# An encoder-decoder layer on one core: where the sum of the last half-size product of a slot stands among its matmuls

## The chip, the cores and the metric

The kernel runs on one core of one Trainium2 chip, as one launch in float32. The metric is device time in microseconds (us). A time is the median of several executions; a profile is one further execution, taken by the hardware profiler. Engines are named as the profile names them: PE is TensorE's matmul, PEld its weight load, DVE is VectorE, ACT is ScalarE, POOL is GpSimd, SP issues the DMAs. Each engine works through its own queue in program order and waits for others by semaphores.

## What is computed

One encoder layer over a short context and one decoder layer over a long sequence:

```python
B, T, S, D, H, DFF = 2, 2048, 77, 512, 16, 2048
def _mha(xq, xkv, w_in, b_in, w_out, b_out, bias):
    q, k, v = (heads(z) for z in (xq @ wq.T + bq, xkv @ wk.T + bk, xkv @ wv.T + bv))
    attn = softmax(q @ k.T / sqrt(hd) + bias)
    return merge(attn @ v) @ w_out.T + b_out
...
memory = encoder_layer(ctx_1024)
yn = _ln(y, dec_n1_s, dec_n1_b)
y = y + _mha(yn, yn, dec_sa_in_w, dec_sa_in_b, dec_sa_out_w, dec_sa_out_b, sb)
y = y + _mha(_ln(y, dec_n2_s, dec_n2_b), memory, dec_ca_in_w, ..., cb)
h = _ln(y, dec_n3_s, dec_n3_b)
y = y + (relu(h @ dec_ff1_w.T + dec_ff1_b) @ dec_ff2_w.T + dec_ff2_b)
```

The part that matters here is the causal self-attention of the decoder (sb is a relative bias plus the causal mask): its projections to q, k, v and its output projection are each a 512 x 512 weight applied to 512 tokens at a time.

## The kernel before

The sequence of each batch is cut into four blocks of 512 tokens, so there are eight blocks (b, m). The self-attention runs as a stream of units (b, m, g, t): a block, a group g of four heads and a tile t of 128 query tokens, 16 units a block and 128 in all. For each unit the scores (line 375) are made in pieces of up to 512 keys, DVE moves them out of PSUM while it takes their maxima (lines 384 and 391), ACT takes the exponentials (line 406), PE turns them (line 427), DVE and ACT copy the turned pieces out (lines 432 and 434), and PE multiplies them by the values (line 456).

All other work of that stage hangs on the units' slots, written out by hand: `jobs` (projections, run in the middle of a slot), `light` (before the jobs) and `late` (behind them). The function `slot(n)` issues them; `last[0]` is true while the last job of a slot is issued. The order in which instructions are issued is the order of each engine's queue; waits between engines are put in by the language that the kernel is written in, from what each instruction reads and writes. A job's weights are loaded to one of three buffers `wqk` a few jobs ahead, in the order of the jobs (`load_next`).

PSUM has eight banks of 512 columns, one tile `psum`. `bank()` hands them out in a ring, less one or so that is kept for the product with the values.

For a block with m > 0 the projections of q, k and v use seven products of half size in place of eight (a scheme of Strassen and Winograd's kind): the 512 x 512 problem is cut in four quarters; sums of weight quarters (S1 to S4) lie in DRAM, sums of token quarters (T1 to T4) are made by POOL. `PARTS` names what each product multiplies. Products are added up one on another in the quarters of the result:

| product | what its sum does |
| --- | --- |
| 1 | starts 11 (by ACT for k, v and output; by DVE with a bias for q) |
| 6 | 12 = 11 + product |
| 7 | 22 = 12 + product (with a step of the bias for q and k) |
| 4 | 21 = 22 + product |
| 2 | added to 11 |
| 5 | added to 12 and to 22 |
| 3 | added to 12 |

- `part_job(kind, b, m, i)` makes one product of k, v or the output ("o"). Its result is one PSUM bank in two halves of 256 columns: four matmuls on line 1134, two for each half (each shows as two records in the profile). Then come the sums, behind all four: lines 1141 and 1145 for product 1, and line 1150 where the job is the last of its slot (half by half, 256 columns each); lines 1155, 1159, 1161 and 1164 else (in one, 512 columns wide, but product 7 of k in two).
- `pair_job(b, m, h, parts)` makes two products of q, or product 3 alone, for the half h of its columns. The two products share a bank, 256 columns each: two matmuls for each on line 1049, and behind all of them the sums (lines 1055 to 1065).

The projections of the output for seven of the eight blocks are part jobs of kind "o" in four slots: products 1 and 6; 7 and 4; 2 and 5; 3. The other slots are in a table, where a and b are the halves of q ("a25" is the pair of products 2 and 5 of half a) and the number is the slot relative to the block's first:

```python
-5: "a16 a74", -4: "k1 k6", -3: "k7 k4", -2: "k2 a25", -1: "k5 k3 a3", 0: "v1 v6", 1: "v7 v4 v2",
2: "v5 v3", 3: "b16", 4: "b74 b25", 5: "b3",
```

For m = 1 the first four rows are three: "k1 a16 k6", "a74 k7", "k4 k2 a25".

Of the kernel before, what the change touches and what calls it, by code (L numbers as in the profile page):

```python
# [54 lines left out]
def tile_encoder_decoder(ctx: ExitStack, tc: tile.TileContext, ins, out):  # L55
# [22 lines left out]
    def vec(name, i):  # L78
        c = _COL[name] + i
        return vecs[:, c : c + 1]  # L80
# [78 lines left out]
    with (  # L159
# [872 lines left out]
        def pair_job(b, m, h, parts):  # L1032

            def load():
                w = sb.tile([P, NC, P], F32, name="wqk", tag="wqk", bufs=3)
                for j, i in enumerate(parts):
                    src = saq_d[Q_OPS.index(PARTS[i][0])][:, ts(h, TOK)]
                    nc.sync.dma_start(w[:, 2 * j : 2 * j + 2, :], src.rearrange("p (k o) -> p k o", k=2))
                return w

            def run(w):
                if parts[0] == 1:
                    for g in (2 * h, 2 * h + 1):
                        qTs[b, m, g] = sb.tile([P, MB], F32, name="q", tag="q", bufs=3)
                mm = bank()
                for j, i in enumerate(parts):
                    n = of_nT(b, m, PARTS[i][1])
                    for c in range(2):
                        nc.tensor.matmul(mm[:, ts(j, TOK)], w[:, 2 * j + c, :], n[:, c, :], start=c == 0, stop=c == 1)  # L1049
                d = {  # L1050
                    f"{r + 1}{c + 1}": qTs[b, m, 2 * h + r][:, ts(c, TOK)] for r in range(2) for c in range(2)
                }
                got = [mm[:, ts(j, TOK)] for j in range(len(parts))]
                if parts == (1, 6):
                    ve.tensor_scalar(d["11"], got[0], qbias[:, 2 * h : 2 * h + 1], None, ALU.add)
                    ve.tensor_tensor(d["12"], got[1], d["11"], ALU.add)
                elif parts == (7, 4):
                    ve.scalar_tensor_tensor(d["22"], got[0], qstep[:, h : h + 1], d["12"], ALU.add, ALU.add)
                    ve.tensor_tensor(d["21"], got[1], d["22"], ALU.add)
                elif parts == (2, 5):  # L1060
                    for to, j in (("11", 0), ("12", 1), ("22", 1)):
                        ve.tensor_tensor(d[to], got[j], d[to], ALU.add)
                else:
                    assert parts == (3,)
                    ve.tensor_tensor(d["12"], got[0], d["12"], ALU.add)

            return load, run, True
        n_tiles, last = {}, [False]
        PARTS = {
            1: ("11", "11"), 2: ("12", "21"), 3: ("S4", "22"), 4: ("22", "T4"),  # L1070
            5: ("S1", "T1"), 6: ("S2", "T2"), 7: ("S3", "T3"),
        }
        ADDS = {2: ("11",), 3: ("12",), 5: ("22", "12")}

        def of_nT(b, m, name):
            if name[0] == "T":
                return n_tiles[b, m][int(name[1]) - 1].rearrange("p (c o) -> p c o", c=2)
            r, c = int(name[0]) - 1, int(name[1]) - 1
            return nTs[b, m][:, 2 * r : 2 * r + 2, ts(c, TOK)]
# [28 lines left out]
        def part_job(kind, b, m, i):  # L1108
            name, by = PARTS[i]

            def load():
                w = sb.tile([P, NC, P], F32, name="wqk", tag="wqk", bufs=3).rearrange("p c o -> p (c o)")
                w = w.rearrange("p (c o) -> p c o", c=2)
                if name[0] == "S":
                    src = sa_d[kind][int(name[1]) - 1].rearrange("p (c o) -> p c o", c=2)
                else:
                    src = quarter(sa_name[kind], int(name[1]) - 1, int(name[0]) - 1, sa_from[kind])
                nc.sync.dma_start(w, src)
                return w

            def place(to):
                r, c = int(to[0]) - 1, int(to[1]) - 1
                if kind == "k":
                    return kT[:, 2 * r : 2 * r + 2, m * MB + c * TOK : m * MB + (c + 1) * TOK]
                if kind == "o":
                    return wbt[:, 2 * c : 2 * c + 2, ts(r, TOK)]
                return vv[:, m * TB + 2 * c : m * TB + 2 * c + 2, ts(r, TOK)]

            def run(w):
                n, mm = of_o(b, m, by) if kind == "o" else of_nT(b, m, by), bank()  # L1130
                left, right = (w, n) if kind == "k" else (n, w)
                for f in range(2):
                    for c in range(2):
                        nc.tensor.matmul(  # L1134
                            mm[:, ts(f, TOK)], left[:, c, ts(f, P)], right[:, c, :], start=c == 0, stop=c == 1,
                        )
                got = mm.rearrange("p (f n) -> p f n", f=2)
                d = {to: place(to) for to in ("11", "12", "21", "22")}
                if i == 1 and kind == "k":
                    for f in range(2):  # L1140
                        nc.scalar.activation(
                            d["11"][:, f, :], got[:, f, :], AF.Identity, bias=vec("dec_sa_in_b", NC + f)
                        )
                elif i == 1:
                    nc.scalar.copy(d["11"], got)
                elif last[0] and not (i == 7 and kind == "k"):
                    for f in range(2):
                        for to in {6: ("12",), 7: ("22",), 4: ("21",)}.get(i) or ADDS[i]:
                            onto = {6: "11", 7: "12", 4: "22"}.get(i, to)
                            ve.tensor_tensor(d[to][:, f, :], got[:, f, :], d[onto][:, f, :], ALU.add)  # L1150
                elif i == 6:
                    ve.tensor_tensor(d["12"], got, d["11"], ALU.add)
                elif i == 7 and kind == "k":
                    for f in range(2):
                        ve.scalar_tensor_tensor(
                            d["22"][:, f, :], got[:, f, :], kstep[:, f : f + 1], d["12"][:, f, :], ALU.add, ALU.add
                        )
                elif i == 7:
                    ve.tensor_tensor(d["22"], got, d["12"], ALU.add)
                elif i == 4:  # L1160
                    ve.tensor_tensor(d["21"], got, d["22"], ALU.add)
                else:
                    for to in ADDS[i]:
                        ve.tensor_tensor(d[to], got, d[to], ALU.add)

            return load, run, True

# [19 lines left out]
        for x, (b, m) in enumerate(blocks):  # L1187
# [3 lines left out]
            if first:  # L1191
                jobs[max(u - 5, -1)].append(q_job(b, m, 0))
                jobs[max(u - 4, -1)].append(k_job(b, m, 0))
                for t, at in enumerate((u + 1, u + 2, u + 3, u + 4) if x else (-1, 1, 3, 4)):
                    jobs[at].append(v_job(b, m, t))
                jobs[u - 1 if x else 0].append(q_job(b, m, 1))
                jobs[u if x else 2].append(k_job(b, m, 1))
                for g, at, then in ((2, 3, 4), (3, 5, 6)) if x else ((2, 6, 7), (3, 8, 9)):
                    jobs[u + at].append(q_job(b, m, g))
                    jobs[u + then].append(k_job(b, m, g))  # L1200
            else:
                todo = {
                    -5: "a16 a74", -4: "k1 k6", -3: "k7 k4", -2: "k2 a25", -1: "k5 k3 a3", 0: "v1 v6", 1: "v7 v4 v2",
                    2: "v5 v3", 3: "b16", 4: "b74 b25", 5: "b3",
                } if x % NMB > 1 else {
                    -4: "k1 a16 k6", -3: "a74 k7", -2: "k4 k2 a25", -1: "k5 k3 a3", 0: "v1 v6", 1: "v7 v4 v2",
                    2: "v5 v3", 3: "b16", 4: "b74 b25", 5: "b3",
                }
                for at, names in todo.items():
                    for name in names.split():  # L1210
                        h, parts = "ab".find(name[0]), tuple(int(i) for i in name[1:])
                        jobs[u + at].append(
                            pair_job(b, m, h, parts) if h >= 0 else part_job(name[0], b, m, parts[0])
                        )
            if x == 0:
                jobs[NU + 5].append(fold_job())
            for t in range(TB):
                end = x == len(blocks) - 1
                out_at = u + NU + (2 if end else 7 if m == NMB - 1 else 6) + t
                if not end:  # L1220
                    if t:
                        continue
                    for k, part in ((0, 1), (0, 6), (1, 7), (1, 4), (2, 2), (2, 5), (3, 3)):
                        jobs[out_at + k].append(part_job("o", b, m, part))
                    late[out_at - 2].append(lambda b=b, m=m: out_sums(b, m))
                    late[out_at].append(lambda b=b, m=m: sum_n("T4", lambda n: of_o(b, m, n)))
# [767 lines left out]
```

## Time and profile before

| | us |
| --- | --- |
| median of 3 runs (2726.21 to 2733.03) | 2726.84 |
| the profiled execution | 2728.59 |
| its span | 2726.8 |

The span runs from the first to the last instruction of the program; the rest of the execution lies around it. The granted clock of PE over the profiled execution was 0.997. In the profile's rows "x8" is a count of instructions, the first number a start and the second a duration in timelines, and what stands in brackets is how long the engine was idle before and who released it. In lists by line, three numbers are the shortest, the median and the longest duration in ns. In lists of waits, the numbers are microseconds in total and how often. A duration that PE shows for a matmul reaches to its modelled end; matmuls overlap, so that the distance of their starts is what each costs.

The stages of the kernel as the trace has them: preparation to about 113 us, the self-attention with the encoder and the first block's cross-attention among it to about 1590 us, then the rest of the cross-attention and the feed-forward to the end.

### The profile page before, as it was taken

What the parts mean: (1) busy time and instruction counts of PE and PEld (TensorE: products, weight loads), DVE (VectorE), ACT (ScalarE), POOL (GpSimd) and SP (SyncE); (2) the same over time, 40 slices, a digit from 0 to 9 for tenths busy, and PEclk for the clock granted to TensorE, in tenths of its full rate; (3) what the DMA queues carried; (4) which work ended last, traced back from release to release, by engine and by line L of the source; (5) the groups of instructions that cost most, each with busy time, mean ns of one, the idle gap of its engine ahead of it and who ended that gap; (6) DMA issues with size and microseconds to landing.
All of it is one profiled execution on the core that took longest, in us unless ns stands there. A gap on an engine that the chain in (4) does not pass through costs nothing.

```text
span 2726.8 us, 68267 instructions
## 1 busy us (share of the span) xinstructions
PE 2708.1 (99%) x26606; PEld 2217.9 (81%) x26606; DVE 1839.9 (67%) x5445; ACT 1537.0 (56%) x2978; POOL 1002.4 (37%) x844
## 2 busy tenths in 40 slices
PE   9999999999999999999999999999999999999998
PEld 6678877777876677777777777898989898989898
DVE  4776688888885677788888783646464746464645
ACT  3554567777786547667777784444444444444431
POOL 2612235500300513322300203455556565656456
PEclk9999999999999999999999999999999999999999
DMA  8724355511213522343311206565657565656465
GB/s 242 213 92 135 126 155 164 168 50 43 67 45 89 143 76 72 111 133 98 126 50 35 79 19 220 171 214 173 213 171 239 168 216 170 218 166 219 151 224 185
DMA packets 296277, 385.10 MB, mean 141 GB/s; under 512 B 41184, under 2 KB 165648, under 8 KB 295826
## 3 DMA queue, kind: packets, MB, share of 16 engines
q1 hardware_dynamic: 295954, 380.73, 44.1%
q8 instruction: 211, 3.46, 0.5%
q14 instruction: 112, 0.92, 0.1%
HBM read 334.15 MB, written 46.47 MB: 140 GB/s over the span
## 4 chain that ended last, share of the span: by engine, by line
PE 95%; DVE 1%; ACT 1%; DMA 1%; POOL 1%; issue 1%; SPq 0%; DVEq 0%; POOLq 0%; ACTq 0%
PE psum L427 18%; PE psum L1638 14%; PE psum L1667 13%; PE psum L375 11%; PE psum L456 9%; PE psum L1134 8%; PE psum L1801 3%; PE psum L1758 3%; PE psum L1049 3%; PE psum L866 2%; PE psum L836 1%; PE psum L874 1%; PE psum L590 1%; PE psum L811 1%; PE psum L239 1%; PE psum L215 1%
## 5 line engine op out<-in xcount | busy, mean ns | idle before, releaser
L406 ACT ACTIVATE pp<-pp,nm 128x128 f32<-128x128 f32 (+15 forms) x512 | 611.8, 1200 | 28.6 <-DVE nm L401 27.8
L384 DVE TENSOR_SCALAR_CACHE_REDUCE pp<-psum 128x512 f32<-128x512 f32 (+3 forms) x1024 | 556.2, 591 | 51.3 <-PE psum L375 49.7
L434 ACT COPY pts<-psum 128x512 f32<-128x512 f32 x714 | 384.1, 594 | 312.6 <-PE psum L427 265.6
L427 PE MATMUL psum<-ident,pp 128*128 128x128 f32 x4352 | 530.4, 277 | 4.7 <-ACT nT L310 4.0
L427 PEld LDWEIGHTS psum<-ident,pp 128*128 128x128 f32 x4352 | 474.0, 141 | 55.7 <-DVE pp L384 21.4
L375 PE MATMUL psum<-kT,q 32*128 32x512 f32 (+3 forms) x2560 | 336.5, 559 | 2.5 <-DVE q L217 1.0
L456 PEld LDWEIGHTS psum<-pts,vv 128*32 128x32 f32 x8704 | 226.4, 110 | 127.4 <-DVE pp L384 55.4
L1667 PE MATMUL psum<-pp 128*128 128x128 f32 x2560 | 304.5, 276 | 1.9 <-POOL pp L962 1.6
L1667 PEld LDWEIGHTS psum<-pp 128*128 128x128 f32 x2560 | 296.3, 192 | 8.6 <-issue 2.8
L432 DVE COPY pts<-psum 128x512 f32<-128x512 f32 x374 | 245.2, 685 | 82.6 <-PE psum L427 80.3
L456 PE MATMUL psum<-pts,vv 128*32 128x128 f32 x8704 | 279.6, 276 | 0.8 <-DVE mx L391 0.3
L962 POOL TENSOR_TENSOR pp<-pp 128x512 f32<-128x512 f32 x159 | 212.8, 1356 | 111.0 <-DMA pp<-in_dec_ff_wT_dram 50.6
L1638 PE MATMUL psum<-vv,pp 128*128 128x256 f32 x1024 | 236.2, 381 | 0.0
L375 PEld LDWEIGHTS psum<-kT,q 32*128 32x128 f32 x2560 | 146.3, 183 | 107.1 <-issue 41.3
L1638 PEld LDWEIGHTS psum<-vv,pp 128*128 128x128 f32 x1024 | 190.3, 190 | 25.8 <-issue 0.5
L391 DVE CUSTOM_DVE_ANT_0 pp<-psum,bias 128x256 f32<-128x256 f32 (+1 forms) x512 | 196.0, 411 | 19.7 <-PE psum L375 19.7
L1651 DVE TENSOR_TENSOR kT<-kT,psum 128x512 f32<-128x512 f32 x96 | 65.8, 686 | 191.6 <-PE psum L1638 191.4
L1654 ACT ACTIVATE kT<-kT,vecs 128x256 f32<-128x256 f32 x192 | 86.9, 501 | 156.6 <-DVE kT L1651 155.9
L1638 PE MATMUL psum<-nT,pp 128*128 128x256 f32 x768 | 174.1, 380 | 0.5 <-DVE oT L471 0.5
L1638 PEld LDWEIGHTS psum<-nT,pp 128*128 128x128 f32 x768 | 144.2, 190 | 20.8 <-issue 1.4
L1675 ACT COPY oT<-psum 128x128 f32<-128x128 f32 x56 | 15.0, 268 | 238.9 <-PE psum L1667 238.9
L494 POOL TENSOR_TENSOR oT<-rirows,oT 128x512 f32<-128x512 f32 x30 | 38.4, 1280 | 293.6 <-DMA rirows<-rec 181.7
(272 smaller groups left out, 4110.6 us busy)
## 6 DMA issues: line engine op xcount, KB each, us to landing
pp<-w_d SPq DMA_DIRECT2D x520, 256.0 KB
pp<-in_dec_ff_wT_dram SPq DMA_DIRECT2D x112, 256.0 KB
bias<-tzg SPq DMA_DIRECT2D x128, 128.0 KB
pp<-wo_d SPq DMA_DIRECT2D x56, 256.0 KB
wqk<-in_dec_sa_in_wT_dram SPq DMA_DIRECT2D x52, 256.0 KB
wqk<-sa_q SPq DMA_DIRECT2D x84, 128.0 KB
vv<-in_enc_ff_wT_dram SPq DMA_DIRECT2D x8, 1024.0 KB
xr<-in_x_dram SPq DMA_DIRECT2D x32, 256.0 KB
```

The lines of the kernel that those rows point to most:

```text
L375: nc.tensor.matmul(banks[r][:, : kn * P], q[rows4(r), ts(t, P)], kT[rows4(r), g, k0 * P : (k0 + kn) * P], start=True, stop=True,)
L384: nc.vector.tensor_scalar(p[:, k0 : k0 + far], s[:, :far], 1.0, None, ALU.mult, ALU.max, accum_out=st["mx"][:, r, c : c + 1],)
L391: nc.vector.tensor_tensor_reduce(p[:, k0 + far : i + 1], s[:, far:kn], near[:, 2 - (kn - far) :], 1.0, LOWEST, ALU.add, ALU.max, accum_out ...
L406: nc.scalar.activation(p, p, AF.Exp, bias=nm, accum_out=to)
L427: nc.tensor.transpose(pt[:, ts(x, P)], state[n]["p"][r][:, k], ident)
L432: nc.vector.tensor_copy(pts[:, : len(load), :], pt[:, :w])
L434: nc.scalar.copy(pts[:, : len(load), :], pt[:, :w])
L456: nc.tensor.matmul(ot[rows4(r)], vv[:, k, ts(g * HC + r, HD)], got.pop((n, k, r)), start=k == k0 and (whole or not begun), stop=k == k1 - ...
L962: engine.tensor_tensor(out, a, b, ALU.subtract)
L1134: nc.tensor.matmul(mm[:, ts(f, TOK)], left[:, c, ts(f, P)], right[:, c, :], start=c == 0, stop=c == 1,)
L1638: nc.tensor.matmul(mm[:, ts(f, TOK)], a[:, c, ts(f, P)], b[:, c, :], start=fresh and f == 0 and c == 0, stop=c == 1, skip_group_check=True,)
L1667: nc.tensor.matmul(psum[:, bank_i, ts(col, P)], lhs[:, c, :], w[:, c, :], start=fresh and k in (0, 3) and c == 0, stop=c == 3, skip_group_ ...
```

## The change

In `part_job`, the sums become an inner function `sums(f)` over a range of halves. Where the job is the last of its slot and is not product 1, the sum of the first half is issued after the first half's two matmuls and ahead of the second half's; the sum of the second half follows its matmuls. Product 7 of k, where it is last, is now handled this way too. Other jobs keep their sums behind all four matmuls, in one.

In `pair_job`, each product's sum is issued right behind its two matmuls, so that the first product's sum stands ahead of the second's matmuls, in every pair.

What each product adds to is now one table, `SUMS`. In pairs, 2 and 5 change places ("a52", "b52"); in slot -2 the pair of q goes ahead of k2, and k2 is then the last; in the output's third slot, 5 goes ahead of 2.

```diff
@@ pair_job
                 mm = bank()
-                for j, i in enumerate(parts):
-                    n = of_nT(b, m, PARTS[i][1])
-                    for c in range(2):
-                        nc.tensor.matmul(mm[:, ts(j, TOK)], w[:, 2 * j + c, :], n[:, c, :], start=c == 0, stop=c == 1)
...
-                got = [mm[:, ts(j, TOK)] for j in range(len(parts))]
-                if parts == (1, 6):
...
+                for j, i in enumerate(parts):
+                    n, got = of_nT(b, m, PARTS[i][1]), mm[:, ts(j, TOK)]
+                    for c in range(2):
+                        nc.tensor.matmul(got, w[:, 2 * j + c, :], n[:, c, :], start=c == 0, stop=c == 1)
+                    if i == 1:
+                        ve.tensor_scalar(d["11"], got, qbias[:, 2 * h : 2 * h + 1], None, ALU.add)
+                    elif i == 7:
+                        ve.scalar_tensor_tensor(d["22"], got, qstep[:, h : h + 1], d["12"], ALU.add, ALU.add)
+                    else:
+                        for to, onto in SUMS[i]:
+                            ve.tensor_tensor(d[to], got, d[onto], ALU.add)
...
+        SUMS = {
+            2: (("11", "11"),), 3: (("12", "12"),), 4: (("21", "22"),), 5: (("12", "12"), ("22", "22")),
+            6: (("12", "11"),), 7: (("22", "12"),),
+        }
@@ part_job
+                def sums(f):
+                    if i == 1 and kind == "k":
+                        for x in range(2)[f]:
+                            bi = vec("dec_sa_in_b", NC + x)
+                            nc.scalar.activation(d["11"][:, x, :], got[:, x, :], AF.Identity, bias=bi)
+                    elif i == 1:
+                        nc.scalar.copy(d["11"][:, f], got[:, f])
+                    elif i == 7 and kind == "k":
+                        for x in range(2)[f]:
+                            ve.scalar_tensor_tensor(
+                                d["22"][:, x, :], got[:, x, :], kstep[:, x : x + 1], d["12"][:, x, :], ALU.add, ALU.add
+                            )
+                    else:
+                        for to, onto in SUMS[i]:
+                            ve.tensor_tensor(d[to][:, f], got[:, f], d[onto][:, f], ALU.add)
+
+                halves = last[0] and i != 1
                 for f in range(2):
                     for c in range(2):
                         nc.tensor.matmul(
                             mm[:, ts(f, TOK)], left[:, c, ts(f, P)], right[:, c, :], start=c == 0, stop=c == 1,
                         )
...
+                    if halves:
+                        sums(slice(f, f + 1))
+                if not halves:
+                    sums(slice(0, 2))
@@ the table of slots
-                    -5: "a16 a74", -4: "k1 k6", -3: "k7 k4", -2: "k2 a25", -1: "k5 k3 a3", 0: "v1 v6", 1: "v7 v4 v2",
-                    2: "v5 v3", 3: "b16", 4: "b74 b25", 5: "b3",
+                    -5: "a16 a74", -4: "k1 k6", -3: "k7 k4", -2: "a52 k2", -1: "k5 k3 a3", 0: "v1 v6", 1: "v7 v4 v2",
+                    2: "v5 v3", 3: "b16", 4: "b74 b52", 5: "b3",
...
-                    -4: "k1 a16 k6", -3: "a74 k7", -2: "k4 k2 a25", -1: "k5 k3 a3", 0: "v1 v6", 1: "v7 v4 v2",
+                    -4: "k1 a16 k6", -3: "a74 k7", -2: "k4 a52 k2", -1: "k5 k3 a3", 0: "v1 v6", 1: "v7 v4 v2",
...
-                    for k, part in ((0, 1), (0, 6), (1, 7), (1, 4), (2, 2), (2, 5), (3, 3)):
+                    for k, part in ((0, 1), (0, 6), (1, 7), (1, 4), (2, 5), (2, 2), (3, 3)):
```

More of the change, by code (lines that the diff above doesn't have):

```diff
@@ L1052, in run @@
                 }
-                got = [mm[:, ts(j, TOK)] for j in range(len(parts))]
-                if parts == (1, 6):
[L1055 to L1065, printed above, removed]
+                for j, i in enumerate(parts):
[9 more added lines that the diff above has]
+                            ve.tensor_tensor(d[to], got, d[onto], ALU.add)
             return load, run, True
         n_tiles, last = {}, [False]
+        SUMS = {
+            2: (("11", "11"),), 3: (("12", "12"),), 4: (("21", "22"),), 5: (("12", "12"), ("22", "22")),
+            6: (("12", "11"),), 7: (("22", "12"),),
+        }
         PARTS = {
@@ L1072, in tile_encoder_decoder @@
         }
-        ADDS = {2: ("11",), 3: ("12",), 5: ("22", "12")}
         def of_nT(b, m, name):
@@ L1131, in run @@
                 left, right = (w, n) if kind == "k" else (n, w)
+                got = mm.rearrange("p (f n) -> p f n", f=2)
+                d = {to: place(to) for to in ("11", "12", "21", "22")}
+                def sums(f):
[14 more added lines that the diff above has]
+                halves = last[0] and i != 1
                 for f in range(2):
@@ L1136, in run @@
                         )
[L1137 to L1164, printed above, removed]
+                    if halves:
+                        sums(slice(f, f + 1))
+                if not halves:
+                    sums(slice(0, 2))
             return load, run, True
@@ L1202, in tile_encoder_decoder @@
                 todo = {
-                    -5: "a16 a74", -4: "k1 k6", -3: "k7 k4", -2: "k2 a25", -1: "k5 k3 a3", 0: "v1 v6", 1: "v7 v4 v2",
-                    2: "v5 v3", 3: "b16", 4: "b74 b25", 5: "b3",
+                    -5: "a16 a74", -4: "k1 k6", -3: "k7 k4", -2: "a52 k2", -1: "k5 k3 a3", 0: "v1 v6", 1: "v7 v4 v2",
+                    2: "v5 v3", 3: "b16", 4: "b74 b52", 5: "b3",
                 } if x % NMB > 1 else {
-                    -4: "k1 a16 k6", -3: "a74 k7", -2: "k4 k2 a25", -1: "k5 k3 a3", 0: "v1 v6", 1: "v7 v4 v2",
-                    2: "v5 v3", 3: "b16", 4: "b74 b25", 5: "b3",
+                    -4: "k1 a16 k6", -3: "a74 k7", -2: "k4 a52 k2", -1: "k5 k3 a3", 0: "v1 v6", 1: "v7 v4 v2",
+                    2: "v5 v3", 3: "b16", 4: "b74 b52", 5: "b3",
                 }
```

## The prediction

> **What bounds the kernel now.** I read the page first (busy times, then the chain of work that ended last), then busy time by stretch, then the timeline of single slots, then the two groups of half-size products and the sums that read them.
>
> ```profile
> span 2726.8 us, 68267 instructions
> PE 2708.1 (99%) x26606; PEld 2217.9 (81%) x26606; DVE 1839.9 (67%) x5445; ACT 1537.0 (56%) x2978; POOL 1002.4 (37%) x844
> PE 95%; DVE 1%; ACT 1%; DMA 1%; POOL 1%; issue 1%; SPq 0%; DVEq 0%; POOLq 0%; ACTq 0%
> ```
>
> PE is the bound from end to end: 99% busy, 95% of the chain. The change touches the attention stage alone, which runs from about 113 to 1590 us. The next three rows are busy time in that stretch: all instructions, then the products of line 1134 alone (k, v and output), then those of line 1049 alone (q).
>
> ```profile
> 113.00:1590.00 1477.00, 1473.93 (x16687) 1137.69 (x16688) 1136.10 (x3897) 1004.22 (x1844) 354.56 (x292) 1.00 0.32 98
> ...
> 113.00:1590.00 1477.00, 242.34 (x1064) 197.13 (x1064) 1.00 0.32 98
> ...
> 113.00:1590.00 1477.00, 78.98 (x336) 62.12 (x336) 1.00 0.32 98
> ```
>
> The columns are PE, PEld, DVE, ACT and POOL busy (in the second and third row PE and PEld). PE is busy 1473.93 of 1477 us, DVE 1136.10 (77%). A microsecond in which PE stands still is therefore a microsecond of the kernel, unless PE would soon have stood still anyway; a microsecond saved on DVE is worth what PE now waits for DVE, and no more.
>
> **Does a sum wait for its half or for the whole bank?** Everything hangs on this, and the trace of before answers it. Here is a slot with three products of v (7, 4, 2), the last of which already has its sum cut in halves.
>
> ```profile
> 1414.86 2.75 PE L1134 MATMUL psum<-wqk,xr 128*128 128x256 f32 x12
> ...
> 1415.92 0.69 DVE L1159 TENSOR_TENSOR vv<-psum,vv 128x512 f32<-128x512 f32 x1 [0.65 <-PE psum L1134]
> ...
> 1417.45 1.89 PE L1134 MATMUL psum<-wqk,nT 128*128 128x256 f32 x8
> 1417.65 0.69 DVE L1161 TENSOR_TENSOR vv<-psum,vv 128x512 f32<-128x512 f32 x1 [1.04 <-PE psum L1134]
> ...
> 1419.44 0.76 DVE L1150 TENSOR_TENSOR vv<-psum,vv 128x256 f32<-128x256 f32 x2 [1.10 <-PE psum L1134]
> ```
>
> A half-size product is 8 matmul records in 1.89 us; each shows 0.379 us, so they follow each other every (1.89 - 0.379) / 7 = 0.216 us, and one half (4 records) takes 0.86 us. The last product runs from 1417.45 to 1419.34. Its first half was complete at 1419.34 - 0.86 = 1418.48, and DVE had been idle since 1418.34. Still the sum of the first half starts at 1419.44, 0.10 us after the last matmul of the second half. In q it is the same:
>
> ```profile
> 1450.67 1.03 PE L1049 MATMUL psum<-nT,wqk 128*128 128x256 f32 x4
> ...
> 1451.53 1.03 PE L1049 MATMUL psum<-xt,wqk 128*128 128x256 f32 x4
> ...
> 1452.67 0.48 DVE L1055 TENSOR_SCALAR q<-psum,qbias 128x256 f32<-128x256 f32 x1 [0.79 <-PE psum L1049]
> 1453.19 0.42 DVE L1056 TENSOR_TENSOR q<-psum,q 128x256 f32<-128x256 f32 x1
> ...
> 1453.67 0.29 PEld L375 LDWEIGHTS psum<-kT,q 32*128 32x128 f32 x2 [0.44 <-DVE q L1056]
> ```
>
> Part 1 was complete at 1451.70 and DVE idle from 1451.88, but its sum (L1055) starts at 1452.67, 0.11 us after part 6's last matmul. So the program makes a reader wait for every earlier writer of the same PSUM bank, not for its own columns. The reverse must then hold too: once a sum is put between the halves, the matmuls of the second half, which write the other columns of that bank, wait until the sum has been read. Today PE never turns to DVE inside a product. After the change it does.
>
> The Trainium skill's "PSUM — Partial Sum Buffer", in "PSUM bank collisions raise a hardware error", says that a matmul writing and VectorE reading the same bank and quadrant at once are an error even on disjoint columns, and that the chip does not hold one of them back. No row here shows a collision; by that rule the wait can't be absent and the first rival below would have no chance at all.
>
> **The stops, counted.** Of q, pairs 16, 74 and 52 have two parts: 3 pairs x 2 halves of the columns x 6 blocks (all but the two with m = 0) = 36 stops. Of k the last product of a slot is 6, then 4 (four blocks) or 7 (two), then 2: 18. Of v it is 6, 2, 3: 18. Of the output it is 6, 4, 2, 3 in seven blocks: 28. Together 100 (of 1064 / 8 = 133 products and 336 / 4 = 84 parts of q). Their price comes from these rows: the half-width sums of line 1150 with what ended their waits and who waited for them, then the two q sums that also add a bias, and one row of products with the shortest, median and longest record.
>
> ```profile
> L1150 DVE TENSOR_TENSOR wbig<-psum,wbig x70: 411/414/426, 232.8 to 1555.0; 128x256 f32<-128x256 f32 x70
> L1150 DVE TENSOR_TENSOR vv<-psum,vv x36: 414/419/426, 159.6 to 1436.7; 128x256 f32<-128x256 f32 x36
> L1150 DVE TENSOR_TENSOR kT<-psum,kT x20: 412/415/425, 119.9 to 1356.6; 128x256 f32<-128x256 f32 x20
>   PE psum L1134: 45.0, 45
>   ACT vv L1145: 12.7, 4
>   ACT wbig L1145: 6.6, 2
>   PEld psum L375: 5.1, 12
> ...
> L1055 DVE TENSOR_SCALAR q<-psum,qbias x12: 476/483/484, 118.1 to 1452.7; 128x256 f32<-128x256 f32 x12
> L1058 DVE SCALAR_TENSOR_TENSOR q<-psum,qstep,q x12: 442/484/484, 125.2 to 1469.2; 128x256 f32<-128x256 f32 x12
> L1134 PE MATMUL psum<-wqk,oT x280: 379/379/483, 229.0 to 1554.3; 128*128 128x256 f32 x140
> ```
>
> **One stop, step by step.** The next matmul would start 0.216 us after the last one of the first half. Now that one must end (0.379 - 0.216 = 0.16 us more), DVE must notice (0.04 to 0.11 in the rows above, 0.08 taken), the sum must run (0.41 us), PE must notice (L1056 ends at 1453.61, the load that waited for it starts at 1453.67: 0.06), and the array starts again without the weight load hidden (483 against 379 ns, the longest record of line 1134 against its median: 0.10). That is 0.81 us. With the 0.48 us sums of L1055 and L1058 it is 0.88. Product 5 of q adds to two places, which takes 0.76 us for two (as the x2 row shows): 1.16.
> 64 x 0.81 + 24 x 0.88 + 12 x 1.16 = 51.8 + 21.1 + 13.9 = **87 us**, if DVE is free each time.
>
> **Where DVE is not free.** PE then waits for what is queued ahead of the sum on DVE. On line 1150, 45 of the 63 first sums waited for PE, 1.00 us in the mean, and their waits ended about 0.08 us after the last matmul; so DVE came free 0.92 us before the product's end in the mean, just as the first half ended (0.86). About half of them came a little later. Three pieces:
> The 13 stops behind a product 5 that is summed whole (v3, and o2 after the swap) have two wide sums ahead, which take 1.29 us here:
>
> ```profile
> 1383.67 1.29 DVE L1164 TENSOR_TENSOR kT<-psum,kT 128x512 f32<-128x512 f32 x2 [0.37 <-PE psum L1134]
> ```
>
> They end 0.08 + 1.29 after product 5, 0.5 us later than the next first half: 13 x 0.5 = 6.5 us. The six waits for ACT's copy of product 1 (12.7 + 6.6 = 19.3 us) were DVE's; now PE stands behind them, less what the half took: 0 to 19.3, 9 taken. The other 81 stops I take at 0.2 us, about a third of one 0.69 us operation left over, with 0 and 0.4 as ends: 16, between 0 and 32. Sum **31 us**, between 6 and 58.
>
> **What comes back.** After the last matmul only one half sum is left instead of two, so DVE is free some 0.38 us earlier (half of 0.76), and the scores that follow, which need the bank or q, wait less. What they wait for now:
>
> ```profile
>   PEld psum L375: 2.7, 6
> ...
>   PEld psum L375: 1.3, 3
> ...
>   PEld psum L375: 0.4, 1
> ...
>   PEld psum L375: 2.0, 5
> ...
> PEld psum L427 <- DVE pp L384: 21.4, 107, 0.3
> ...
> PEld psum L375 <- DVE pts L432: 14.5, 64, 0.3
> ```
>
> The first four rows are who waited for lines 1164, 1056, 1059 and 1062; with 5.1 for line 1150 they make 11.5 us, all that can come back directly. The last two are waits of the whole kernel for other DVE work, which shrink as DVE and ACT catch up while PE stands: at most 21.4 + 14.5 = 36 more. I take **-15 us**, between 0 and -47.
>
> **The swaps.** Putting 5 before 2 (and k2 after a52) moves no matmul count. The sums change width: in the output product 5 goes from four half sums to two wide ones and product 2 from one wide to two halves, k2 from one to two; that is tenths of a microsecond on DVE in 13 slots, hidden beside PE at 77% DVE. The weight loads keep their number and size; in 13 slots two of them trade places in SP's queue, and in 12 pairs the two half loads of one tile do. No load of these weights shows among PE's waits and the DMA engines are busy 0.32 of the stretch, so I cost this at nothing; with that cover gone a 256 KB load at the stretch's 98 GB/s is 2.6 us, x 25 = 65 us.
>
> **The sum.** 87 + 31 - 15 = +103 us. The profiled execution took 2728.59 us (span 2726.8 and 1.8 around it), 1.75 above the median of 2726.84. 2728.59 + 103 = 2831.6; against the median 2829.8. I predict **2830 us**. The ends: 87 + 6 - 47 = +46 (2773) and 87 + 58 - 0 = +145 (2872).
>
> **Rivals.**
> *No wait (the other side).* If the program kept its waits by columns, or if the new place of the sum changed nothing that an engine sees (PE and DVE have queues of their own, and each keeps its own order), PE would run through and each last sum would end 0.38 us earlier. The place is every last product; the gain ends at the 11.5 us of direct waits: 2715 to 2727, not slower. It decides if a first half's sum starts before the second half's matmuls are done. Against it stand both timelines: an idle DVE did not start early. Chance 0.06, of which 0.02 by more than 0.3%.
> *PE would have waited anyway.* If the scores' waits for banks are far larger than the releasers show, because the matmul records swallow them, each stop is paid back within its slot. Then half of the 87 returns besides the 47: +46 - 43 = +3 at the lowest, so 2732 to 2773, 2752 in the middle. For it: the 0.44 us wait above stands right behind a product. Against: 1473.93 of 1477 busy. Chance 0.08.
> *DVE late at every stop.* The stops stretch each slot, so a stop could meet DVE with a full wide sum or a copy ahead each time: 100 x 0.69 + 87 = +156, 2883 and up. For it: the 18 of 63 sums on line 1150 that did not wait for PE. Against: as PE falls back DVE catches up. Chance 0.05.
>
> **Chances and range.** Forecast 0.81 (2773 to 2872), no wait 0.06, paid back 0.08, DVE late 0.05. The range is 2773 to 2872. About 0.3% (8 us) is what this kernel's measurement can tell from no change. Faster 0.02, same 0.04, slower 0.94.
>
> **What will show it.** Right: in the stretch PE's busy time stays near 1474 us while the stretch grows to about 1580; the lines of the half-size products show waits for DVE of their own sums, about 100 of some 0.7 us; the first sums start about 0.1 us after the fourth matmul record, not the eighth; some 100 more matmul records are long. The scores' waits for the last sums are shorter. Wrong: first sums that start while PE writes the second half; or the stops there and the span hardly longer, with the waits of lines 375 and 427 gone; or stops of over 1.5 us in the mean, which would put the growth above 145.

## The result, and the profile after

| | median us | ratio to before | 95% interval |
| --- | --- | --- | --- |
| before | 2726.76 (2726.21 to 2733.03, 4 runs) | 1 | |
| changed | 2839.04 (2836.45 to 2840.31, 4 runs) | 1.0405 | 1.0387 to 1.0423 |

The changed kernel is 112 us slower; 103 us were forecast. The page of the changed kernel has, beside the rows shown before, the row of the scores (line 375); its counterpart of before follows in a fence of its own. In these rows the numbers behind the bar are busy microseconds and the mean nanoseconds of one, then idle time.

```profile
span 2838.1 us, 68318 instructions
...
PE 2725.8 (96%) x26606; PEld 2205.9 (78%) x26606; DVE 1848.2 (65%) x5444; ACT 1535.9 (54%) x2978; POOL 1000.3 (35%) x844
...
L375 PE MATMUL psum<-kT,q 32*128 32x512 f32 (+3 forms) x2560 | 322.2, 566 | 4.6 <-DVE q L217 2.1 <-ACT kT L231 1.4 <-ACT nT L310 0.5
```

```profile
L375 PE MATMUL psum<-kT,q 32*128 32x512 f32 (+3 forms) x2560 | 336.5, 559 | 2.5 <-DVE q L217 1.0
```

PE has the same 26606 matmul records and has fallen from 99 to 96% of the span. The busy time by stretch shows where. The stretch of the changed kernel is cut at 1700 us, where PE has done about as much as it had at 1590 us before (16675 and 16687 records). The last scores lie a little past both marks: they start at 1628.0 us before and at 1739.4 us now.

```profile
113.00:1700.00 1587.00, 1491.27 (x16675) 1123.90 (x16676) 1144.23 (x3896) 1003.14 (x1843) 354.07 (x292) 0.99 0.30 91
```

PE stands still for 1587 - 1491.27 = 96 us of that stretch; it was 1477 - 1473.93 = 3 us before. DVE, ACT and POOL do what they did (1144 against 1136, 1003 against 1004, 354 against 355 us). Who makes PE wait is told by the view of waits of the changed kernel, for PE (total us, times, longest):

```profile
PE psum L1151 <- DVE wbig L1146: 26.3, 28, 3.8
PE psum L1151 <- DVE vv L1146: 20.9, 18, 3.4
PE psum L1052 <- DVE q L1059: 14.3, 12, 2.0
PE psum L1151 <- DVE kT L1146: 8.8, 16, 0.6
PE psum L1052 <- issue: 8.6, 8, 3.8
PE psum L1052 <- DVE q L1056: 6.0, 6, 1.5
PE psum L1052 <- DVE q L1054: 4.0, 6, 0.9
...
PE psum L1052 <- POOL pp L962: 1.2, 2, 0.6
PE psum L1151 <- DVE kT L1141: 1.2, 2, 0.6
...
PE psum L1052 <- POOL vv L962: 0.6, 1, 0.6
PE psum L1052 <- POOL xr L962: 0.6, 1, 0.6
```

Lines 1151 and 1052 are the products of k, v and output and of q, 1146 and 1141 and 1054 to 1059 their sums. The rows on line 1151 count 28 + 18 + 16 + 2 = 64 waits, those on 1052 12 + 8 + 6 + 6 + 2 + 1 + 1 = 36: the 100 stops, one by one, 92.5 us together. (In twelve of them the view names POOL or nothing, where by its place it is a stop like the others.) Before, neither line waited for a sum of its own.

One stop from the timeline of the changed kernel, in the last product of a v slot as shown for the kernel before (start, duration):

```profile
1522.89 1.03 PE L1151 MATMUL psum<-wqk,nT 128*128 128x256 f32 x4
1523.10 0.69 DVE L1146 TENSOR_TENSOR vv<-psum,vv 128x512 f32<-128x512 f32 x1 [1.03 <-PE psum L1151]
1524.03 0.42 DVE L1146 TENSOR_TENSOR vv<-psum,vv 128x256 f32<-128x256 f32 x1 [0.24 <-PE psum L1151]
1524.51 0.73 PEld L1151 LDWEIGHTS psum<-wqk,nT 128*128 128x128 f32 x4 [0.99 <-DVE vv L1146]
1524.51 1.13 PE L1151 MATMUL psum<-wqk,nT 128*128 128x256 f32 x4 [0.59 <-DVE vv L1146]
...
1525.68 0.43 DVE L1146 TENSOR_TENSOR vv<-psum,vv 128x256 f32<-128x256 f32 x1 [1.22 <-PE psum L1151]
```

The first half's matmuls end at 1523.92; DVE, which is idle, starts the sum at 1524.03 (0.11); it ends at 1524.45; PE starts at 1524.51 (0.06); the four matmuls take 1.13 in place of 1.03 (0.10). With the 0.16 us by which matmuls overlap otherwise the stop is 0.11 + 0.42 + 0.06 + 0.10 + 0.16 = 0.85 us. In q:

```profile
1557.95 1.03 PE L1052 MATMUL psum<-nT,wqk 128*128 128x256 f32 x4
1559.09 0.48 DVE L1054 TENSOR_SCALAR q<-psum,qbias 128x256 f32<-128x256 f32 x1
...
1559.63 1.13 PE L1052 MATMUL psum<-xt,wqk 128*128 128x256 f32 x4 [0.65 <-DVE q L1054]
```

The same steps with a 0.48 us sum: 0.65 + 0.10 + 0.16 = 0.91.

From the starts of the matmul records each of the 100 stops can be measured, as what the two distances behind a first half have above 0.216 us each. They add up to 120.3 us (jobs of one name together; o is the output):

```
products of k, v, output: k2 6 stops 5.2 us, k4 4 3.1, k6 6 5.6, k7 2 1.7, v2 6 4.9, v3 6 8.5, v6 6 12.6,
                          o2 7 9.4, o3 7 7.9, o4 7 6.0, o6 7 10.5                         64 stops, 75.4 us
q:                        16 12 14.5, 74 12 12.8, 52 12 17.4                              36 stops, 44.8 us
```

Some of it comes back: the scores are busy 336.5 - 322.2 = 14.3 us less. The distances from start to start within their groups fell alike, from 234.3 to 219.2 us together. That these were waits for a bank or an operand, which the overlapping records show as busy time, is read from this and not shown by a run. 120 - 14 = 106 of the 112 us.

Most of the rest is the clock. Over the profiled execution PE was granted 0.993 of its clock, and 0.997 before. The trace gives the clock in stretches: full, or half, as here (start and duration; then the row of busy times, with the clock third from the end):

```profile
1007.34 2.04 PE L1052 MATMUL psum<-xt,wqk 128*128 128x256 f32 x4 [3.78 <-issue]
1009.18 1.91 PE L1151 MATMUL psum<-xt,wqk 128*128 128x256 f32 x4
1006.00:1015.50 9.50, 7.57 (x34) 4.79 (x37) 3.04 (x9) 0.00 (x0) 0.00 (x0) 0.50 0.30 80
```

Four records take 1.91 us in place of 1.03, and they start 0.427 us apart in place of 0.216. At half clock half of PE's busy time is lost: 15.3 us in all, against 6.8 before, 8.5 us more. About 1.4 of these lie within the stops as measured, so some 7 us come on top: 106 + 7 = 113. This is an estimate from the trace's clock and PE's records. The six longest stops (2.3 to 4.3 us) each have a half-clock stretch that begins between 1.7 us before PE's restart and 1.3 us after it; no stop under 2 us has one of its own. That the long stops bring the half clock is likely from this, but it is not shown: no run was made for it, and in experiment 6 a stop of 2.9 us has no such stretch.

### The profile page after: what moved, and what is told of

Read it like the earlier page. It is cut to its first block, busy times and chain, and to the rows that moved or that the text cites. A ratio compares the mean times of both kernels' runs of the same rounds, so it can differ in the third digit from the quotient of the medians.

```text
span 2838.1 us, 68318 instructions
## 1 busy us (share of the span) xinstructions
PE 2725.8 (96%) x26606; PEld 2205.9 (78%) x26606; DVE 1848.2 (65%) x5444; ACT 1535.9 (54%) x2978; POOL 1000.3 (35%) x844
## 4 chain that ended last, share of the span: by engine, by line
PE 49%; DVE 1%; POOL 1%; issue 0%; ACT 0%; DVEq 0%; POOLq 0%; ACTq 0%
PE psum L1631 14%; PE psum L1660 12%; PE psum L427 5%; PE psum L1794 3%; PE psum L1751 3%; PE psum L375 3%; PE psum L456 2%; PE psum L866 2%; PE psum L1151 1%; PE psum L836 1%; PE psum L874 1%; PE psum L811 1%; DVE pp L384 1%; PE psum L251 0%; PE psum L1052 0%
## 5 line engine op out<-in xcount | busy, mean ns | idle before, releaser
L375 PE MATMUL psum<-kT,q 32*128 32x512 f32 (+3 forms) x2560 | 322.2, 566 | 4.6 <-DVE q L217 2.1
L375 PEld LDWEIGHTS psum<-kT,q 32*128 32x128 f32 x2560 | 140.2, 186 | 99.9 <-issue 46.6
```

The source lines that it names most:

```text
L375: nc.tensor.matmul(banks[r][:, : kn * P], q[rows4(r), ts(t, P)], kT[rows4(r), g, k0 * P : (k0 + kn) * P], start=True, stop=True,)
```

## The experiments

The theory: the half sums and the matmuls behind them use one PSUM bank, the program's waits go by bank, so PE stops 100 times. Rival A: the orders that were changed along with it cost the time. Rival B: it is the narrow sums and the turns between engines, whatever the bank. Rival C: few of the stops matter. All kernels below were compared with the kernel before on the same chip; the medians of the kernel before were 2728.09 (runs 1 to 4) and 2727.10 us (runs 5 to 8).

**1. The orders alone.** The kernel before, with

```diff
-                    -2: "k2 a25" ... 4: "b74 b25"
+                    -2: "a52 k2" ... 4: "b74 b52"
-                elif parts == (2, 5):
-                    for to, j in (("11", 0), ("12", 1), ("22", 1)):
+                elif parts == (5, 2):
+                    for to, j in (("12", 0), ("22", 0), ("11", 1)):
-                    for k, part in (..., (2, 2), (2, 5), (3, 3)):
+                    for k, part in (..., (2, 5), (2, 2), (3, 3)):
```

> The kernel before with only the changed orders (52 for 25, the pair of q ahead of k2, 5 ahead of 2 in the output), all sums behind all matmuls of their bank. Theory (the time goes into PE's waits inside a product, because a sum and the second half's matmuls share a PSUM bank): no stop arises, 2727 +/- 4 us. Rival A (the orders themselves cost: weight loads that trade places, sums that come late): 2737 us or more, a good part of the 112.

2726.18 us, ratio 0.9995 (0.9986 to 1.0004). The orders cost nothing that can be measured. Rival A falls.

**2. Stops in k, v and output alone.** The changed kernel, with q as before:

```diff
                     for c in range(2):
                         nc.tensor.matmul(got, w[:, 2 * j + c, :], n[:, c, :], start=c == 0, stop=c == 1)
+                for j, i in enumerate(parts):
+                    got = mm[:, ts(j, TOK)]
                     if i == 1:
```

> The changed kernel, but in q both products' sums stand behind all four matmuls again. 64 stops are left, those of k, v and output, which measure 75.4 us in the changed kernel's trace (the excess of the two matmul distances behind each first half over 0.216 us). Theory: 75 less some 6 that come back in later waits, 2796 us, between 2788 and 2802. Rival A (orders): 2839 less little. Rival C (the stops overlap with waits that were there anyway, and what is lost is lost in few places): less than 40 us over before.

2802.55 us, ratio 1.0274 (1.0260 to 1.0288): 74.5 us over before. That is just above the interval that was given. In this run's own trace the 64 stops measure 78.6 us, 3 more than in the changed kernel's. Rival C, with less than 40 us, falls for these stops.

**3. Stops in q alone.**

```diff
-                    if halves:
-                        sums(slice(f, f + 1))
-                if not halves:
-                    sums(slice(0, 2))
+                for f in (slice(0, 1), slice(1, 2)) if halves else (slice(0, 2),):
+                    sums(f)
```

> The changed kernel, but the half sums of k, v and output stand behind all four matmuls again. 36 stops are left, 44.8 us in the changed kernel's trace. Theory: 45 less some 3, 2769 us, between 2762 and 2773; with the run of parts alone the two gains over before add up to 111. Rival A: as for parts alone. Rival C: the sum of the two is well above or below 111.

2769.72 us, ratio 1.0152 (1.0138 to 1.0166): 41.6 us over before. 74.5 + 41.6 = 116 against 112 for both: the parts add up, and the 4 us between them lie within the intervals. That two groups add up does not by itself say that most stops cost; the stops measured one by one do, none of them under 0.78 us.

**4. The same instructions, two banks.** This is the run that decides. Nothing moves in the queues of PE or DVE; the second half's product (and the second product of a pair) is written to another bank:

```diff
-                mm = bank()
+                mms = [bank() for _ in parts]
-                    n, got = of_nT(b, m, PARTS[i][1]), mm[:, ts(j, TOK)]
+                    n, got = of_nT(b, m, PARTS[i][1]), mms[j][:, :TOK]
...
+                mms = [mm, bank()] if halves else [mm, mm]
+                        g = mms[f.start].rearrange("p (f n) -> p f n", f=2) if halves else got
-                            mm[:, ts(f, TOK)], left[:, c, ts(f, P)], right[:, c, :], start=c == 0, stop=c == 1,
+                            mms[f][:, ts(f, TOK)], left[:, c, ts(f, P)], right[:, c, :], start=c == 0, stop=c == 1,
```

> The changed kernel, with the same instructions in the same order on PE and DVE, but the second half's product (and the second product of a pair) goes to a bank of its own. Theory: no matmul writes a bank that a sum still reads, all 100 stops are gone, and each last sum ends earlier: 2715 to 2729 us; the ring hands out 100 more banks, so scores may meet a busy bank a little sooner, up to 2735. Rival B (the time is in the narrow sums and in PE and DVE taking turns, whatever the bank): 2800 or more.

2722.35 us, ratio 0.9981 (0.9972 to 0.9990): all of the loss is gone, and the kernel is 5.7 us faster than before. Its timeline at the same place (lines 1153 and 1149 are the products and sums here):

```profile
1416.19 1.89 PE L1153 MATMUL psum<-wqk,nT 128*128 128x256 f32 x8
1416.39 0.69 DVE L1149 TENSOR_TENSOR vv<-psum,vv 128x512 f32<-128x512 f32 x1 [1.03 <-PE psum L1153]
1417.33 0.42 DVE L1149 TENSOR_TENSOR vv<-psum,vv 128x256 f32<-128x256 f32 x1 [0.24 <-PE psum L1153]
...
1418.19 0.42 DVE L1149 TENSOR_TENSOR vv<-psum,vv 128x256 f32<-128x256 f32 x1 [0.44 <-PE psum L1153]
```

The eight matmuls run through in 1.89 us to 1418.08, and the first half's sum starts at 1417.33, in the midst of them. DVE does the same sum in the same 0.42 us, in the same order. Only the banks differ, so the shared bank is the cause; rival B falls. For a read of PSUM while a matmul runs, the Trainium skill's "PSUM — Partial Sum Buffer", in "Summary: rules for kernel authors", wants a different bank, or at least a different quadrant. The page says so because of collisions, of which no run here shows one; what the traces add is the price of one bank with its guard in place: 100 stops with one bank, none with two.

**5. More stops.** If stops cost what the prediction put down for them, 50 more cost in proportion. The changed kernel, with

```diff
-                halves = last[0] and i != 1
+                halves = i != 1
```

> The changed kernel with the halves taken in every product of k, v and output but product 1, not only in the last of a slot: 50 stops more, 31 behind a sum to one place and 19 behind product 5's two. Theory: by the prediction's prices 31 x 0.81 + 19 x 1.16 = 47 us and some 0.3 us each for a DVE that comes late, 60 us in all: 2899 us, between 2885 and 2915. Rival C (only few stops cost, where DVE is behind): less than 25 us more.

2901.34 us, ratio 1.0641 (1.0625 to 1.0657), 62.3 us over the changed kernel where 60 were expected. In its own trace the stops of k, v and output measure 137.3 us, 62 more than the 75.4 of the changed kernel. The view of waits counts 42 + 36 + 30 + 6 = 114 = 64 + 50 on line 1151:

```profile
PE psum L1151 <- DVE wbig L1146: 39.1, 42, 3.8
PE psum L1151 <- DVE vv L1146: 34.9, 36, 3.5
PE psum L1151 <- DVE kT L1146: 27.0, 30, 5.2
...
PE psum L1151 <- DVE kT L1141: 3.5, 6, 0.6
```

**6. What makes some stops long.** Inside a v6 or o6 a stop is 1.78 us in the mean. Product 6 adds to 11, which ACT copies from product 1. The longest of the output's stops in the changed kernel:

```profile
952.86 1.48 ACT L310 ACTIVATE nT<-psum,vecs 128x128 f32<-128x128 f32 x4
954.22 1.50 ACT L814 ACTIVATE pp<-psum,vecs 128x128 f32<-128x128 f32 x4
955.59 0.60 ACT L1138 COPY wbig<-psum 128x512 f32<-128x512 f32 x1
956.28 0.42 DVE L1146 TENSOR_TENSOR wbig<-psum,wbig 128x256 f32<-128x256 f32 x1 [4.63 <-ACT wbig L1138]
956.76 1.13 PE L1151 MATMUL psum<-wqk,xr 128*128 128x256 f32 x4 [3.83 <-DVE wbig L1146]
```

ACT comes to its copy (line 1138) at 955.59, behind its other work. With DVE as copier:

```diff
-                        nc.scalar.copy(d["11"][:, f], got[:, f])
+                        ve.tensor_copy(d["11"][:, f], got[:, f])
```

> The changed kernel, but product 1 of v and output is copied by DVE in place of ACT (13 copies of 512 columns). The 13 stops behind a v6 or o6 measure 23.1 us in the changed kernel's trace, 1.78 each. Theory (the part of them above 0.81 us is ACT, busy with exponentials, that copies product 1 late): they fall to 13 x 0.81 = 10.5, so 12 us less, 2827 us, between 2823 and 2831. Rival D (it is DVE's own backlog): 2839 us or more, since DVE gets 13 operations of 0.69 us on top.

2824.59 us, ratio 1.0364 (1.0344 to 1.0385), some 14 us less than the changed kernel. As the whole explanation rival D falls, but it holds in part. By the starts of the records the 13 stops fell from 23.1 to 14.5 us, 8.6 less and not 12. The six of v6 fell from 12.6 to 5.8. Of the seven of o6 one fell from 4.10 to 0.84 and one from 1.90 to 0.79, but four grew, from 0.84 to 1.02 us each to 1.17 to 1.81: there DVE comes late itself (in the first of them its copy waits behind the layer norm of lines 282 to 285). So the total came out near the forecast in part by luck. The clock can account for the other 6 us: by the same reckoning as above the half clock cost 3.1 us in the profiled execution of this run, and 15.3 in that of the changed kernel. The four executions of this run had 0.994 to 0.998 of the clock, and the one at 0.994 took 2835.1 us, 3 us less than the changed kernel's 2838.2 us at 0.994. The rows of waits on line 1151 are now:

```profile
PE psum L1151 <- DVE wbig L1146: 24.5, 28, 1.5
PE psum L1151 <- DVE vv L1146: 14.4, 18, 2.7
...
PE psum L1151 <- DVE kT L1146: 8.8, 16, 0.6
```

Against the changed kernel the longest waits for the output's and v's sums fell from 3.8 and 3.4 to 1.5 and 2.7 us. In both of these ACT had come late to its copy, and not for exponentials of the self-attention alone: it had work of lines 310 and 814 ahead of one copy, and of lines 867 and 849 ahead of the other.

**7 and 8. Which of the two gains by its second bank?** Two banks for k, v and output with q summed behind both products, and the reverse (two banks in q, half sums of the others behind all four matmuls).

> As with two banks, for k, v and output alone; in q both products share a bank and both sums stand behind. Theory: no stops; the gain of the early first half, if it is made in the 64 products that end a slot, is here: 2720 to 2725 us. If it is made in q: 2726 to 2729.

> As with two banks, for q alone; the half sums of k, v and output stand behind all four matmuls in one bank. Theory: no stops, and the other part of the gain: 2726 to 2729 us if the gain is made in the products that end a slot, 2720 to 2725 if it is made in q.

2723.61 us, ratio 0.9982 (0.9973 to 0.9990), and 2722.29 us, ratio 0.9984 (0.9975 to 0.9993). Neither of the two answers came: each gains as much alone as both do together. Three intervals that overlap this far don't tell whose gain it is; that stays open. The clock leaves room for gains that add up: the executions with two banks everywhere had 0.9973 of it in the mean, these two runs 0.9983 and 0.9980, the kernel before 0.9987. At 2.7 us for each 0.001 (a thousandth of 2722 us, since PE is busy throughout) the gains at an equal clock would be some 9.5, 4.6 and 6.7 us. That is an estimate, and no run held the clock still. As measured, any of the three is faster than the kernel before by 0.16 to 0.19%.

## Why the prediction was right

**The wait goes by bank.** This was read off two places in the trace of before in which an idle DVE let a finished half lie. The reverse wait, that of the matmuls for the sum, was inferred. The changed trace shows it 100 times, and experiment 4 takes it away by a second bank alone.

**The price of a stop.** 0.81, 0.88 and 1.16 us were put together from single rows (overlap lost, notice, sum, notice, restart). The stops in which DVE is free measure 0.78 to 0.85, 0.84 to 0.92 and 1.11 to 1.19 us. No step of a stop was missing.

**DVE late.** 31 us was taken; 120.3 - 87 = 33 was measured. Of its pieces the 13 stops behind product 5 measure 17.9 us (v3 and o2), 17.9 - 13 x 0.81 = 7.4 where 6.5 was worked out. For the copies by ACT 9 was taken; v6 and o6 lie 23.1 - 13 x 0.81 = 12.6 above the price of a stop, of which experiment 6 takes 8.6 away, as a balance of shorter and longer stops. That leaves 33.3 - 7.4 - 12.6 = 13.3 for the other 81 stops, where 16 was taken. One reading beneath these terms was off: the "63 first sums" of line 1150 belong to 56 products, because product 5 of the output has two places to add to. Of the 56 first sums, 45 waited for PE and six for ACT, so DVE was free more often than "18 of 63" says.

**What comes back.** 15 us was taken, and the scores' busy time fell by 14.3. The mechanism was right in its direct part: the waits of the scores' weight loads for these sums, 11.5 us before, are down to 1.4. The 3.5 us more were sought in the wrong place: the two rows of other waits, 21.4 and 14.5 us, stand at 21.1 and 14.7. In experiment 4, which has no stop, the scores' busy time is 325.9 us, 10.6 less than before: most of what comes back is owed to sums that end earlier, not to the stops. What the scores lost beyond that is not explained.

**The swaps.** They were put at nothing; alone they measured a ratio of 0.9995, no change.

**The sum.** +103 us was forecast, +112 came. The stops measure 120 where 118 were put down, and 14 come back where 15 were; that makes 106. The term that the prediction does not have is the clock: PE's busy time in the stretch was to stay near 1474 us and came to 1491, and some 7 us of the whole are lost at half clock, beside and behind the longest stops. The executions of the changed kernel had 0.993 to 0.995 of the clock, those of the kernel before in the experiments 0.996 to 1.000.

**The rivals.** None came. PE did not run through (experiment 4 shows what that would have been, 2722, inside the 2715 to 2727 put down for it). The stops were not paid back within their slots. DVE was not late at each: the stops come to 120 us, not 156. One end was reckoned unevenly: the 2732 of the second rival starts from the profiled execution, the other ends from the median, from which it is 2730; nothing hangs on it.

## What to carry to other kernels

In this program a PSUM bank is the unit of waiting between PE and its readers. To sum the first half of a product while the second half is made, give the second half a bank of its own; the order on each engine need not change. On a kernel that PE bounds, count each place in which another engine's read is put between two matmuls of one bank, and price it as lost overlap, two notices, the read and the restart (0.8 us here with a 0.41 us read), plus what stands ahead of the read on its engine. Then look at the granted clock: here it fell beside the longest stops. An idle reader in the trace that lets finished columns lie is the sign that waits go by bank.

## What was not expected

That 14.3 us could go from the busy time of the scores without a change in their number: their records overlap, so that busy time can hold waits. That the gain of two banks measures some 5 us whether k, v and output have them, or q, or all. And that the six longest of the 100 stops stand beside all of the time at half clock in the stretch of the attention.
